# A graph layer's message stage in a written order, with its statistics taken by pairs of PSUM banks

## The chip, the cores and the metric

The kernel runs on one core of one Trainium2 chip. Everything is float32. The metric is the device time of one execution in microseconds; 4303.69 us is the median of three runs before the change (4302.92 to 4304.81). PE is the matrix engine, PEld its weight loads, DVE the vector engine, ACT the scalar engine, POOL the GpSimd engine, and SP the engine that here only issues DMAs.

## The reference

There are 12500 nodes with 96 features and 412500 edges with four attributes, sorted by target node `dst`. A small layer makes a message for each edge, the messages are added up at their targets, and each row of the result is normalized.

```python
def _mlp(h, W, b, gamma, beta):
    h = relu(h @ W + b)
    mu = mean(h, axis=0)
    var = mean(square(h - mu), axis=0)
    return gamma * (h - mu) * rsqrt(var + EPS) + beta

node_feat = _mlp(x, W_node, b_node, g_node, beta_node)
edge_feat = _mlp(edge_attr, W_edge, b_edge, g_edge, beta_edge)
message = concatenate([x[src], x[dst], edge_feat], axis=1)       # 412500 x 288
message = _mlp(message, W_msg, b_msg, g_msg, beta_msg)
agg = segment_sum(message, dst, num_segments=12500)
out = layernorm(x + agg + node_feat)
```

The two batch normalizations over all edges need their mean and variance before anything that comes after them can be scaled. The edge one must be known before the messages; the message one can be applied at the end, to the sums.

## The kernel before

**Tables.** The product with the message weights is split in three: x times the source part gives `p_tab`, x times the target part gives `q_tab`, both tables in DRAM with 12544 rows of 96 (function `table`, lines 136 to 152). Each table is made in seven chunks of 14 matmuls; a chunk's results go to four PSUM banks, `pt`, four matmuls to a bank and two in the last. DVE and ACT copy the banks in turn into `trow`, and a DMA writes the chunk. Both tables have four `pt` buffers. ACT's queue has the four `rel_d` writes of line 200 between the two tables, and DVE works on what they write.

**Gathers.** Edges are handled in tiles of 128; four tiles are a group (512 edges, 806 groups, the last with three tiles), four groups a block (202 blocks). For each tile POOL issues one indirect DMA (line 289, `gather`), which fetches 128 rows of `p_tab` by source node. Two kinds of buffers take them. The first 26 blocks are gathered early, in two staging buffers of 16 gathers each, and SP writes each to DRAM (`spill`, line 303). Later groups go to a ring of 30 group buffers (`ahead_of`); a ring buffer is free again when DVE has added it into `hs` (line 377).

**What sets the order early on.** Lines 308 to 324 write out the order of SP and POOL by hand: four chunks of `q_tab`, spill, three chunks, three spills, then the node stage (`nodes`) with two spills in it, then the edge statistics (`edge_norm`), where four of each five load steps are followed by a spill. A staging buffer can be filled again when its spill has landed. The other three engines are ordered by a scheduler.

**Edge statistics.** For each of 202 blocks three matmuls of ten rows (line 249) make the four groups' edge features packed in 128 rows, in a PSUM tile of three banks with two buffers; ACT applies relu to all three banks at once (line 252) and DVE takes mean and variance of each bank (line 254). The three matmuls use different row groups of the array.

**Message stage.** Per block, `load` fetches edge attributes and the four 30-row windows of `q_tab` that the groups' targets fall in; `prepare` makes edge features `pr` (line 362, a matmul of six rows for each group, four banks) and from them the operand `left` (ACT line 364, DVE line 365). Per group, `message` makes `z` (line 371, four matmuls), a one-hot matrix of the targets (373), the sum with the gathered rows (377) and its relu into `h` (378); `reduce`, one group later, multiplies `h` with itself and the one-hot matrix into `pa` (386) and adds the two parts into the 30 columns of `agg` (389) and into `gram` (390). DVE and SP read the window's first column into registers in `load` (349). In this stage the scheduler orders all engines. The spilled blocks are read back (404) and stand evenly among the late ones.

**End.** From `gram` come the message mean and variance; lines 598 to 631 finish the rows.

Of the kernel before, what the change touches and what calls it, by code (L numbers as in the profile page):

```python
# [14 lines left out]
OP = mybir.AluOpType  # L15
# [39 lines left out]
RING = 30  # L55
J = 8
# [14 lines left out]
def gnn(ctx, tc, t):  # L71
# [64 lines left out]
    def table(out, w, work, ps, queues):  # L136

        rows = out.rearrange("(p b) f -> p b f", b=NB)
        for c in range(0, NB, CH):
            r = work.tile([P, CH, C], F32, name="trow", bufs=3)  # L140
            for j, i in enumerate(range(0, CH, NBK)):
                n = min(NBK, CH - i)
                pt = ps.tile([P, NBK, C], F32, name="pt", bufs=4)
                for g in range(n):
                    k = COL[c + i + g]
                    nc.tensor.matmul(pt[:, g, :], xp[:, k:k + P], w, start=True, stop=True)  # L146
                if j % 2:
                    nc.scalar.activation(r[:, i:i + n, :], pt[:, :n, :], AF.Copy)  # L148
                else:
                    nc.vector.tensor_copy(r[:, i:i + n, :], pt[:, :n, :])  # L150
            queues[c // CH % len(queues)].dma_start(rows[:, c:c + CH, :], r)
            yield

    with tc.tile_pool(name="win_w", bufs=1) as work, tc.tile_pool(name="win_ps", bufs=2, space=PSUM) as ps:
        for _ in table(p_tab, w_msg[:, 0, :], work, ps, (nc.sync, nc.scalar)):
            pass
# [77 lines left out]
    def edge_norm():  # L234

        with tc.tile_pool(name="es", bufs=2) as work, tc.tile_pool(name="es1", bufs=1) as one, \
                tc.tile_pool(name="es_ps", bufs=2, space=PSUM) as ps:
            stats = one.tile([P, NS, NBL, 6], F32, name="estats")
            for b in range(NBL):
                if b % J == 0:  # L240
                    yield
                    ea = work.tile([P, J, GE], F32, name="ea")
                    n = min(J, NBL - b)
                    for i in range(NS):
                        nc.sync.dma_start(ea[Q * i:Q * i + 2 * EK, :n, :],
                                          t["ea"][EK * i:EK * (i + 2), b:b + n, :])
                pr = ps.tile([P, NS, GE], F32, name="pr")
                for i in range(NS):
                    nc.tensor.matmul(pr[:, i, :], wide[Q * i:Q * i + 2 * EK, :],  # L249
                                     ea[Q * i:Q * i + 2 * EK, b % J, :], start=True, stop=True)  # L250
                r = work.tile([P, NS, GE], F32, name="r")
                nc.scalar.activation(r, pr, AF.Relu)  # L252
                for i in range(NS):
                    nc.vector.bn_stats(stats[:, i, b, :], r[:, i, :])  # L254
# [30 lines left out]
    def fast(ring):  # L285
# [22 lines left out]
        with tc.manual_schedule(engines={ET.SP, ET.Pool}):  # L308
            with tc.tile_pool(name="tab_w", bufs=1) as work, tc.tile_pool(name="tab_ps", bufs=2, space=PSUM) as ps:
                for i, _ in enumerate(table(q_tab, w_msg[:, 1, :], work, ps, (nc.sync,))):  # L310
                    if i in (3, 6):
                        next(store)
# [12 lines left out]

        with tc.tile_pool(name="fix", bufs=1) as fix, tc.tile_pool(name="msg", bufs=2) as work, \
# [3 lines left out]
            rhs = fix.tile([P, 2, BG, C], F32, name="rhs")  # L330
            nc.vector.tensor_copy(rhs[:C], w_e[:, None, None, :].to_broadcast([C, 2, BG, C]))
            for i in range(2):
# [5 lines left out]
            hb = [fix.tile([P, GT, P], F32, name=f"h{i}") for i in range(4)]  # L338
# [3 lines left out]
            def load(s, b):  # L342

                n = min(BG, NG - b * BG)
                ea = work.tile([P, GE], F32, name="ea")
# [4 lines left out]
                    base[:, b * BG:(b + 1) * BG], engines=[ET.DVE, ET.SP], min_val=0, max_val=N - 1,  # L350
                    skip_runtime_bounds_check_because="they are nodes' numbers")
                for i in range(n):
                    nc.sync.dma_start(rhs[C:C + WN, s % 2, i, :], q_tab[bass.ds(val[i], WN), :])
                return ea, val

            def prepare(s, b, ea):

                n = min(BG, NG - b * BG)
                x = left[s % 2]
                pr = ps.tile([C + WN, BG, GE], F32, name="pr", bufs=1)  # L360
                for i in range(n):
                    nc.tensor.matmul(pr[:, i, :], we[Q * i:Q * i + EK + 1, :],  # L362
                                     ea[Q * i:Q * i + EK + 1, :], start=True, stop=True)
                nc.scalar.activation(x[:C, :n, :], pr[:C, :n, :], AF.Relu)  # L364
                nc.vector.tensor_scalar(x[C:C + WN, :n, :], pr[C:, :n, :], 0.0, None, op0=OP.is_equal)  # L365

            def message(s, g, h, pg):
                n = min(GT, NT - g * GT)
                z = ps.tile([P, GT, C], F32, name="z")
                for i in range(n):  # L370
                    nc.tensor.matmul(z[:, i, :], left[s % 2][:KR, g % BG, i * P:(i + 1) * P],  # L371
                                     rhs[:KR, s % 2, g % BG, :], start=True, stop=True)
# [7 lines left out]
            def reduce(g, h, val):  # L380

                n = min(GT, NT - g * GT)
                pa = ps.tile([C + 1, P], F32, name="pa")
# [4 lines left out]
                to = agg[:, bass.ds(val, WN)]  # L388
# [4 lines left out]
            early, late = list(range(SPILL // BG)), list(range(SPILL // BG, NBL))  # L393
            order = []
            for i, b in enumerate(late):
                order.append(b)
                while early and (SPILL // BG - len(early)) * len(late) < i * (SPILL // BG):
                    order.append(early.pop(0))
            order += early

            def fetch(b):
                if b * BG < SPILL:
                    back = work.tile([P, BG, GT, C], F32, name="pb")
                    nc.sync.dma_start(back, spill[b].rearrange("p g (a c) -> p g a c", a=GT))
                    for i in range(BG):
                        got[b * BG + i] = back[:, i, :, :]

            ea, val = load(0, order[0])
            prepare(0, order[0], ea)
            fetch(order[0])  # L410
            last, n, ahead = None, 0, SPILL + RING
            for s, b in enumerate(order):
                more = s + 1 < len(order)
                if more:
                    ea, then = load(s + 1, order[s + 1])
                    fetch(order[s + 1])
                for g in range(b * BG, min((b + 1) * BG, NG)):
                    if g % BG == 1 and more:
                        prepare(s + 1, order[s + 1], ea)
                    h = hb[n % len(hb)]  # L420
                    n += 1
                    message(s, g, h, got.pop(g))
                    if last:
                        reduce(*last)
                    last = g, h, val[g % BG]
                    if g >= SPILL and ahead < NG:
                        got[ahead] = ahead_of(ahead)
                        ahead += 1
                val = then
            reduce(*last)  # L430
# [237 lines left out]
```

## Time and profile before

| | |
|---|---|
| median of three runs | 4303.69 us |
| the profiled execution | 5713.74 us |
| its span, first to last instruction | 5712.0 us |
| mean granted PE clock in the span | 0.656 |
| busy: PE, PEld, DVE, ACT, POOL | 3507.9, 2613.4, 1830.5, 1126.2, 3070.7 us |
| message stage, from about 1230 to 5649 us: busy PE, DVE, ACT, POOL | 2898.6, 1311.6, 774.9, 2556.7 us |
| edge statistics, from about 400 to 1230 us: busy PE, DVE, ACT, POOL | 404.0, 395.1, 292.5, 397.6 us |
| granted clock in these two | 0.67 and 0.50 |
| DMA: mean rate | 55 GB/s |

In a group row the number after x is the count, then come busy time and the mean of one in nanoseconds, then the idle time of the engine just before these instructions and what ended it ("issue": nothing that the profile shows; "remote": a semaphore whose setter it cannot name). A row of waits gives the total, how often, and the longest. A row of the timeline gives start, duration, engine, line and operation, with the idle time before it in brackets. A float32 matmul leaves two records of PE. The profiled execution is a third longer than the runs without the profiler.

### The profile page before, as it was taken

Reading aid. Unit: us, or ns where it says so; the run is one execution under the profiler, and the core shown is the slowest. Engines: PE = TensorE matmul, PEld = TensorE weight load, DVE = VectorE, ACT = ScalarE, POOL = GpSimd, SP = SyncE. Lnnn points to the kernel's source line nnn. Section 1 sums busy time; section 2 is a strip of 40 time slices with the busy share of each in tenths; the row PEclk is TensorE's granted clock in tenths of the full one; section 3 lists DMA queues with packets and bytes.
Section 4 is the critical chain, followed back from the end, with each engine's and each line's share of the span. In section 5 each row is a group of like instructions: output and inputs, shape, how many; then the busy total and the mean of one; then the engine's idle time right before and its main releaser. Section 6 shows DMA issues by size and latency. Waiting matters only on the chain. (4 is left out here: it accounts for less than half of the span.)

```text
span 5712.0 us, 52958 instructions
## 1 busy us (share of the span) xinstructions
PE 3507.9 (61%) x16561; PEld 2613.4 (46%) x16561; DVE 1830.5 (32%) x4227; ACT 1126.2 (20%) x1304; POOL 3070.7 (54%) x3231
## 2 busy tenths in 40 slices
PE   3445666146666666766667566676566666665768
PEld 3331111024545455555555455455455555554547
DVE  1134555142323223232222232232322222322326
ACT  0113444021111111111111111111111111111113
POOL 2254444725555565555565555655555655556550
PEclk9955555557776666566666766666666666666667
DMA  3232323212222222222222222222222222222212
GB/s 117 73 97 56 70 63 68 47 42 51 52 52 49 46 50 52 50 52 49 52 46 51 50 51 49 47 52 49 51 50 52 46 50 52 49 52 46 50 44 82
DMA packets 190423, 315.48 MB, mean 55 GB/s; under 512 B 95817, under 2 KB 96201, under 8 KB 189128
## 3 DMA queue, kind: packets, MB, share of 16 engines
q0 software_dynamic: 103136, 158.62, 13.2%
q1 hardware_dynamic: 83502, 141.01, 8.9%
q10 hardware_dynamic: 3496, 12.36, 0.7%
q8 instruction: 137, 2.24, 0.2%
q14 instruction: 152, 1.25, 0.1%
HBM read 270.34 MB, written 41.37 MB: 55 GB/s over the span
## 5 line engine op out<-in xcount | busy, mean ns | idle before, releaser
L289 POOL DMA_INDIRECT pg<-p_tab,src x2807 | 2670.2, 951 | 1884.8 <-issue 787.5
L371 PE MATMUL z<-rhs,left 127*128 127x96 f32 x6446 | 1330.3, 350 | 706.3 <-issue 385.0
L371 PEld LDWEIGHTS z<-rhs,left 127*128 127x128 f32 x6446 | 1181.7, 261 | 1158.2 <-issue 684.0
L386 PE MATMUL pa<-h 128*97 128x127 f32 x6446 | 1236.4, 355 | 656.2 <-issue 351.7
L386 PEld LDWEIGHTS pa<-h 128*97 128x97 f32 x6446 | 1077.7, 230 | 719.8 <-issue 377.2
L378 ACT ACTIVATE h<-hs 128x384 f32<-128x384 f32 x806 | 419.5, 521 | 3094.3 <-DVE hs L377 1528.7
L389 DVE TENSOR_TENSOR agg<-pa,agg 97x30 f32 x806 | 150.4, 187 | 1978.1 <-PE z L371 752.6
L377 DVE TENSOR_TENSOR hs<-z,pg 128x384 f32<-128x384 f32 x702 | 390.2, 556 | 1054.7 <-issue 471.4
L289 POOL DMA_INDIRECT stage<-p_tab,src x416 | 399.6, 961 | 608.1 <-DMA spill<-stage 428.3
L362 PE MATMUL pr<-ea,we 6*126 6x512 f32 x1612 | 601.4, 841 | 157.4 <-issue 102.5
L249 PE MATMUL pr<-ea,wide 10*128 10x512 f32 x1212 | 406.6, 1107 | 409.2 <-ACT r L252 264.8
L254 DVE BATCH_NORM_STATS2 estats<-r 128x6 f32<-128x512 f32 x606 | 372.1, 680 | 442.6 <-ACT r L252 287.2
L364 ACT ACTIVATE left<-pr 96x2048 f32<-96x2048 f32 x202 | 376.3, 1863 | 549.9 <-remote 260.7
L365 DVE TENSOR_SCALAR left<-pr 30x2048 f32<-30x2048 f32 x202 | 462.9, 2292 | 43.8 <-ACT left L364 37.6
L249 PEld LDWEIGHTS pr<-ea,wide 10*128 10x128 f32 x1212 | 114.5, 307 | 700.0 <-ACT r L252 484.4
L252 ACT ACTIVATE r<-pr 128x1536 f32<-128x1536 f32 x202 | 292.2, 1451 | 592.9 <-remote 384.4
L362 PEld LDWEIGHTS pr<-ea,we 6*126 6x126 f32 x1612 | 150.6, 232 | 226.0 <-issue 150.3
L373 DVE TENSOR_TENSOR h<-rel,iota 128x120 f32<-128x120 f32 x806 | 204.9, 275 | 2.4 <-issue 0.4
L390 DVE TENSOR_TENSOR gram<-pa,gram 97x97 f32<-97x97 f32 x806 | 201.8, 250 | 0.3 <-DVE agg L389 0.3
L146 PE MATMUL pt<-w_msg,xp 96*128 96x96 f32 x392 | 85.6, 423 | 139.2 <-ACT trow L148 131.4
L146 PEld LDWEIGHTS pt<-w_msg,xp 96*128 96x128 f32 x392 | 84.1, 332 | 140.5 <-ACT trow L148 132.2
L223 PE MATMUL py<-center,xp 96*128 96x96 f32 x196 | 43.1, 423 | 60.5 <-DVE y0s L227 37.5
(95 smaller groups left out, 443.5 us busy)
## 6 DMA issues: line engine op xcount, KB each, us to landing
ea<-in_eaq SPq DMA_DIRECT2D x202, 256.0 KB
pg<-p_tab,src POOLq DMA_INDIRECT x2807
spill<-stage SPq DMA_DIRECT2D x26, 768.0 KB
pb<-spill SPq DMA_DIRECT2D x26, 768.0 KB
rhs<-q_tab SPq DMA_DIRECT2D x806, 11.2 KB
ea<-in_ea SPq DMA_DIRECT2D x75, 160.0 KB
stage<-p_tab,src POOLq DMA_INDIRECT x416
q_tab<-trow SPq DMA_DIRECT2D x7, 672.0 KB
```

The lines of the kernel that those rows point to most:

```text
L249: nc.tensor.matmul(pr[:, i, :], wide[Q * i:Q * i + 2 * EK, :], ea[Q * i:Q * i + 2 * EK, b % J, :], start=True, stop=True)
L252: nc.scalar.activation(r, pr, AF.Relu)
L254: nc.vector.bn_stats(stats[:, i, b, :], r[:, i, :])
L289: nc.gpsimd.indirect_dma_start(out=pg[:, i, :], out_offset=None, in_=p_tab[:, :], in_offset=bass.IndirectOffsetOnAxis(ap=src[:, k:k + 1], ...
L362: nc.tensor.matmul(pr[:, i, :], we[Q * i:Q * i + EK + 1, :], ea[Q * i:Q * i + EK + 1, :], start=True, stop=True)
L364: nc.scalar.activation(x[:C, :n, :], pr[:C, :n, :], AF.Relu)
L365: nc.vector.tensor_scalar(x[C:C + WN, :n, :], pr[C:, :n, :], 0.0, None, op0=OP.is_equal)
L371: nc.tensor.matmul(z[:, i, :], left[s % 2][:KR, g % BG, i * P:(i + 1) * P], rhs[:KR, s % 2, g % BG, :], start=True, stop=True)
L373: nc.vector.tensor_tensor(h[:, :, C + 1:C + 1 + WN], rel[:, g, :].unsqueeze(2).to_broadcast([P, GT, WN]), iota[:, None, :].to_broadcast([P ...
L377: nc.vector.tensor_add(hs[:, :n, :], z[:, :n, :], pg[:, :n, :])
L378: nc.scalar.activation(h[:, :n, :C], hs[:, :n, :], AF.Relu)
L386: nc.tensor.matmul(pa[:, :C + 1 + WN], h[:r, i, :C + 1], h[:r, i, :C + 1 + WN], start=i == 0, stop=i == n - 1)
```

## The change

The message stage is put in an order written by hand for all five engines. Edge features of a block are made during the block before it, all four matmuls in one step (`edges`), and `left` is made from them in two halves (`prepare`). `load` runs two blocks ahead, with three `ea` and three `rhs` buffers; `h` has six buffers instead of four. `linear` makes z one group ahead. `sums` puts the sums of four groups in one PSUM bank, and `add` adds a group's sums to `agg` and `gram` five groups later (`SKEW`); DVE reads its registers there. The edge statistics take consecutive matmuls by pairs, two banks to a PSUM tile with four buffers, so that ACT works on 1024 columns at a time. The second table, `q_tab`, gets eight `pt` buffers; `p_tab` keeps four.

```diff
+SKEW = 5
+HB, RB = 6, 3
...
-    def table(out, w, work, ps, queues):
+    def table(out, w, work, ps, queues, bufs):
...
-                pt = ps.tile([P, NBK, C], F32, name="pt", bufs=4)
+                pt = ps.tile([P, NBK, C], F32, name="pt", bufs=bufs)
...
-        for _ in table(p_tab, w_msg[:, 0, :], work, ps, (nc.sync, nc.scalar)):
+        for _ in table(p_tab, w_msg[:, 0, :], work, ps, (nc.sync, nc.scalar), 4):
...
-                tc.tile_pool(name="es_ps", bufs=2, space=PSUM) as ps:
+                tc.tile_pool(name="es_ps", bufs=4, space=PSUM) as ps:
...
-                pr = ps.tile([P, NS, GE], F32, name="pr")
                 for i in range(NS):
-                    nc.tensor.matmul(pr[:, i, :], wide[Q * i:Q * i + 2 * EK, :],
+                    k = NS * b + i
+                    if k % 2 == 0:
+                        pr = ps.tile([P, 2, GE], F32, name="pr")
+                    nc.tensor.matmul(pr[:, k % 2, :], wide[Q * i:Q * i + 2 * EK, :],
                                      ea[Q * i:Q * i + 2 * EK, b % J, :], start=True, stop=True)
-                r = work.tile([P, NS, GE], F32, name="r")
-                nc.scalar.activation(r, pr, AF.Relu)
-                for i in range(NS):
-                    nc.vector.bn_stats(stats[:, i, b, :], r[:, i, :])
+                    if k % 2:
+                        r = work.tile([P, 2, GE], F32, name="r", bufs=4)
+                        nc.scalar.activation(r, pr, AF.Relu)
+                        for o in (1, 0):
+                            nc.vector.bn_stats(stats[:, (k - o) % NS, (k - o) // NS, :], r[:, 1 - o, :])
...
-                for i, _ in enumerate(table(q_tab, w_msg[:, 1, :], work, ps, (nc.sync,))):
+                for i, _ in enumerate(table(q_tab, w_msg[:, 1, :], work, ps, (nc.sync,), 8)):
...
+            def edges(s):
+
+                prs[s] = ps.tile([C + WN, BG, GE], F32, name="pr", bufs=1)
+                for i in range(min(BG, NG - order[s] * BG)):
+                    nc.tensor.matmul(prs[s][:, i, :], we[Q * i:Q * i + EK + 1, :],
+                                     eas[s][Q * i:Q * i + EK + 1, :], start=True, stop=True)
+
+            def prepare(s, i):
+
+                part = slice(i, min(i + BG // 2, NG - order[s] * BG))
+                if part.start < part.stop:
+                    pr, x = prs[s], left[s % 2]
+                    nc.scalar.activation(x[:C, part, :], pr[:C, part, :], AF.Relu)
+                    nc.vector.tensor_scalar(x[C:C + WN, part, :], pr[C:, part, :], 0.0, None, op0=OP.is_equal)
...
+            def sums(k):
+
+                g = steps[k][1]
                 n = min(GT, NT - g * GT)
-                pa = ps.tile([C + 1, P], F32, name="pa")
+                h = hb[k % HB]
+                if k % 4 == 0:
+                    pas[k // 4] = ps.tile([C + 1, 4, P], F32, name="pa")
+                pa = pas[k // 4][:, k % 4, :]
...
+            def add(k):
+                s, g = steps[k]
+                if s not in vals:
+                    b = order[s]
+                    _, vals[s] = nc.values_load_multi_w_load_instructions(
+                        base[:, b * BG:(b + 1) * BG], engines=[ET.DVE], min_val=0, max_val=N - 1,
+                        skip_runtime_bounds_check_because="they are nodes' numbers")
+                pa = pas[k // 4][:, k % 4, :]
+                to = agg[:, bass.ds(vals[s][g % BG], WN)]
                 nc.vector.tensor_tensor(to, pa[:, C + 1:C + 1 + WN], to, op=OP.add)
                 nc.vector.tensor_add(gram, pa[:, :C + 1], gram)
...
+            with tc.manual_schedule(engines={ET.SP, ET.Pool, ET.PE, ET.DVE, ET.Activation}):
+                load(0)
+                fetch(0)
+                load(1)
+                edges(0)
+                prepare(0, 0)
+                prepare(0, BG // 2)
+                linear(0)
+                for k in range(n + SKEW):
+                    s, g = steps[min(k, n - 1)]
+                    if k < n and g % BG == 0:
+                        if s + 2 < len(order):
+                            load(s + 2)
+                        if s + 1 < len(order):
+                            fetch(s + 1)
+                    if k + 1 < n:
+                        linear(k + 1)
+                    if k < n:
+                        message(k)
+                    if 0 <= k - 1 < n:
+                        sums(k - 1)
+                    if k < n and s + 1 < len(order):
+                        if g % BG == 0:
+                            edges(s + 1)
+                        if g % BG >= BG // 2:
+                            prepare(s + 1, (g % BG - BG // 2) * (BG // 2))
+                    if k >= SKEW:
+                        add(k - SKEW)
+                    if k < n and g >= SPILL and ahead < NG:
                         got[ahead] = ahead_of(ahead)
                         ahead += 1
```

## The prediction

> **What bounds the kernel now.** I read the page's busy times and groups first, then the waits of POOL, then stretches of the timeline.
>
> ```profile
> PE 3507.9 (61%) x16561; PEld 2613.4 (46%) x16561; DVE 1830.5 (32%) x4227; ACT 1126.2 (20%) x1304; POOL 3070.7 (54%) x3231
> ...
> L289 POOL DMA_INDIRECT pg<-p_tab,src x2807 | 2670.2, 951 | 1884.8 <-issue 787.5
> ...
> L289 POOL DMA_INDIRECT stage<-p_tab,src x416 | 399.6, 961 | 608.1 <-DMA spill<-stage 428.3
> ```
>
> Nothing looks full: POOL is busy for 54%. But its 2807 + 416 = 3223 gathers are one serial list, and 787.5 us of their idle time ended on "issue", on nothing. The waits say how often, and what else stopped POOL:
>
> ```profile
> POOL pg L289 <- issue: 787.5, 2499, 2.7
> POOL pg L289 <- DVE h L373: 584.2, 83, 15.6
> POOL stage L289 <- DMA spill<-stage: 428.3, 13, 137.7
> ```
>
> 787.5 / 2499 = 0.32 us before nearly every gather. In the timeline:
>
> ```profile
> 3007.30 0.95 POOL L289 DMA_INDIRECT pg<-p_tab,src  x1 [0.30 <-issue]
> 3008.55 0.95 POOL L289 DMA_INDIRECT pg<-p_tab,src  x1 [0.30 <-issue]
> 3009.80 0.95 POOL L289 DMA_INDIRECT pg<-p_tab,src  x1 [0.30 <-issue]
> ```
>
> A gather costs POOL 1.25 us from start to start. **A rule against a row**: the Trainium skill (Perfetto Trace Analysis, "GPSIMD Engine Instruction") says that the span shown for a GpSimd instruction is unreliable, and to time it by start-to-start spacing. By the row's 951 ns the gathers are 3065 us, 71% of the 4303.69 us median, and POOL has slack; by the spacing they are 3223 x 1.25 = 4029 us, 94% of it, and POOL is the bound. I take the spacing.
>
> **The profiled execution against the median.** It took 5713.74 us, 1410 more than 4303.69. POOL's list explains both. Its 33rd gather starts at 236.21; 3191 more take 3191 x 1.25 = 3989; after the last the kernel needs about 5 us for the last group (eviction 0.56, relu 0.52, sums 1.0, adds 0.44, landing about 2) and 63.5 us from the last add (5648.5) to the span's end, and 1.7 us lie around the span. That is 236 + 3989 + 5 + 63.5 + 1.7 = 4295: 9 us below the median. In the profiled execution the last gather starts at 5563, so POOL also waited 5563 - 236 - 3989 = 1338 us, and its ring of 30 groups was full, so that the end took 149 us and not 69. 1338 + 80 = 1418 is the excess of 1410, but for those 9 us. The waits come from stretches like this one, in which DVE, PE and SP stand still together and POOL alone goes on until its ring is full:
>
> ```profile
> 3003.39 0.47 DVE L373 TENSOR_TENSOR h<-rel,iota 128x120 f32<-128x120 f32 x2
> 3016.31 0.19 DVE L389 TENSOR_TENSOR agg<-pa,agg 97x30 f32 x1 [12.45 <-remote]
> ```
>
> I count these stops to the profiled execution alone: with them POOL could not have finished in 4304 us. Without gathers beside it, at the end of the stage, the message work runs free:
>
> ```profile
> 5641.85 0.55 DVE L377 TENSOR_TENSOR hs<-z,pg 128x384 f32<-128x384 f32 x1
> ...
> 5643.15 0.56 DVE L377 TENSOR_TENSOR hs<-z,pg 128x384 f32<-128x384 f32 x1 [0.29 <-PE z L371]
> ...
> 5644.94 0.56 DVE L377 TENSOR_TENSOR hs<-z,pg 128x384 f32<-128x384 f32 x1 [0.34 <-PE z L371]
> ```
>
> About 1.6 us a group, where POOL needs 4 x 1.25 = 5.0. Of 806 groups, 672 are gathered in the stage (104 come from the spill, 30 from the ring), so POOL's pace is 672 x 5.0 / 806 = 4.17 us a group. So I read the measured kernel as POOL-bound from 236 us on; the message work has to stay under 4.17.
>
> **The change part by part.**
>
> *Written order of the message stage.* The same 806 groups. PE per group, by the spacing of the records' starts in the timeline: z is 8 records at 0.111 us with the full clock granted (0.213 with half), pa 8 at 0.108 (0.211). The edge features pr come as three matmuls together and one alone now, two passes over the array of 1.06 us each (2.06 at half); the change issues all four together: one. Per group before 0.89 + 0.86 + 2 x 1.06/4 = 2.3 us (half clock 4.4), after 2.0 (3.9). All of that lies beside gathers: cost of the cut 0. Without that cover it would be worth 202 x 1.06 = 214 to 202 x 2.06 = 416 us.
>
> *Halves of left.* Two ACT operations of 1.02 (the 1024-wide form, minimum of that group) for one of 1.86: +0.18 a block; DVE 2 x 1.23 for 2.29: +0.17. 202 x 0.18 = 36 us each, on engines busy for 20% and 32%: 0; at worst 36 without cover.
>
> *Adds five groups later, four sums in a bank.* Same instructions, no new DMA; a DVE register load now stands directly before its first use (0.34 us, 202 times, 69 us beside gathers: 0). With a fixed order, what waits blocks its queue: hs(k) waits on DVE for the gather, behind it stand the half of left and the add of k-5; PE's pr of the next block waits for left's last half, and behind it z(k+2). Each is needed two groups later, 10 us at POOL's pace, and the chain is 0.52 + 1.02 + 1.23 + 1.0 = 3.8. At the end four more adds follow the last one: 4 x 0.44 = 1.8, partly under the last relu and sums: 0.3 to 1.8, I take +1.
>
> *SP.* Per block the same six DMAs and one register load, a block earlier, with a third rhs and ea buffer; 12 bias rows for 8 (4 x 0.33 us, before the stage, while the ring fills: 0). POOL's list keeps its order, and each ring gather waits for the same eviction as now.
>
> *Statistics by pairs.* ACT per 1024 columns: from 1451 ns (1536) and 1863 (2048) 0.80 ns a column, so 1.04; 303 x 1.04 = 315 against 293. DVE keeps 606 operations at 0.6 us spacing, 1.8 us a block. Before, undisturbed:
>
> ```profile
> 574.56 1.45 ACT L252 ACTIVATE r<-pr 128x1536 f32<-128x1536 f32 x1 [0.20 <-PE pr L249]
> 576.60 1.45 ACT L252 ACTIVATE r<-pr 128x1536 f32<-128x1536 f32 x1 [0.59 <-PE pr L249]
> 578.30 1.45 ACT L252 ACTIVATE r<-pr 128x1536 f32<-128x1536 f32 x1 [0.26 <-PE pr L249]
> ```
>
> Two blocks in 3.7 us, 1.85 each. Four of five load steps (8 blocks) also spill 16 gathers: 40 blocks take 74 us, POOL's 64 gathers 80. POOL sets the pace, with 8% to spare: 0.
>
> *Eight banks for the target table.* This part is on POOL's path. POOL stands from 98 to 236 us for the first spill, which SP issues after four q_tab writes:
>
> ```profile
> 74.74 6.29 PE L146 MATMUL pt<-w_msg,xp 96*128 96x96 f32 x28 [0.37 <-DVE most L188]
> ...
> 211.96 24.42 PE L146 MATMUL pt<-w_msg,xp 96*128 96x96 f32 x113 [130.93 <-ACT trow L148]
> 212.38 18.54 SPq L151 DMA_DIRECT2D q_tab<-trow  x4
> ...
> 231.21 0.33 SPq L303 DMA_DIRECT2D spill<-stage  x1
> ...
> 236.21 0.95 POOL L289 DMA_INDIRECT stage<-p_tab,src  x1 [137.68 <-DMA spill<-stage]
> ```
>
> At 74.74 PE fills its four banks (28 records, 14 matmuls, one of seven chunks) and waits until 211.96 for ACT. With eight banks it fills two chunks, so 14 matmuls fewer stand between 211.96 and the fourth write: 28 records x 0.216 us = 6.0 us. Here too a **rule and a row** differ: the skill (TensorE: Matmul & The Clock Gate, "What's actually happening") has the clock go full after about 3.4 us of sustained work; then it would be nearer 28 x 0.11 = 3.1. The row shows 113 records in 24.42 us without a break, 0.216 each to the end, so 6.0. What follows (second spill, node stage, statistics) starts 6 us sooner with it.
>
> Sum: 4303.7 - 6.0 + 1 = 4298.7; 4298.
>
> **Rivals.** A, as above: 4298, own range 4293 to 4304; 0.48. A measurement of this kernel can tell about 0.2%, 8.6 us, from no change.
>
> B, the 9 us that the sum leaves, and more if a gather is a little cheaper unprofiled, are POOL waits for slow message or statistics work, and the change removes part: 4280 to 4294, say 4289. For it: POOL waits for DVE are the profile's largest; against: they belong to the stops. 0.20.
>
> C, gathers are much cheaper unprofiled (0.95: chain 236 + 3031 + 70 = 3337) and message work at half clock is the bound: 806 x 4.4 + 750 + 65 = 4361, near the median. Then pr in one pass gives 806 x 3.9 + 815 = 3958. For it: granted clock 0.67 in the stage; against: the spacing never varies, whatever else runs. 0.10.
>
> D, slower: the pairs break the three-fold overlap of the statistics matmuls on PE. Two at a time at half clock is about 1.71 us a pair, 1.5 pairs 2.56 a block; 40 blocks take 102 us against 80 of gathers, SP's spills come late, and POOL waits 22 us in each of 4.75 such rounds: +107, 4405. It decides from 80/40 = 2.0 us a block on; at 2.1 it is 4 x 4.75 = +19, 4317. Against: with four buffers PE need not stop between pairs. 0.22.
>
> **How the numbers follow.** Faster: C, nine tenths of B and a little of A (0.15): 0.10 + 0.18 + 0.07 = 0.35. Slower is D, 0.22; the rest, 0.43, is the same. The range takes in A, B, a gather cheaper by 0.01 us with its 32 us of freed waits, and the lower third of D: 4270 to 4330.
>
> **What would show it.** Gathers still 1.25 us apart; the first POOL gather after the long wait at 230 and not 236; pr as four records side by side; less PE busy time and no shorter total. It is wrong if the spacing changes, if POOL waits for spills in the statistics grow, or if the median falls below 4270, which POOL's list forbids.

## The result, and the profile after

The changed kernel takes 4322.25 us (median of 5 runs, 4319.65 to 4325.15) against 4302.92 for the kernel before (5 runs, 4300.59 to 4304.81): a ratio of 1.0048, 95% interval 1.0036 to 1.0059. It is 19 us slower. The forecast was 4298, "the same" the likeliest; the range 4270 to 4330 held the time, the direction was wrong.

Each of the five sets of experiments below ran on one chip with the kernel before beside it, whose median was 4302 and 4313 us in two sets and 5665 to 5718 us in three, with the stretches in which DVE, PE and SP stand still, so a kernel is compared only with the kernel before of its own set.

The profile of the changed kernel is free of those stretches. Its page:

```profile
span 4323.2 us, 52620 instructions
...
PE 2815.2 (65%) x16561; PEld 2342.0 (54%) x16561; DVE 1849.7 (43%) x4430; ACT 1141.2 (26%) x1606; POOL 3068.5 (71%) x3231
...
L294 POOL DMA_INDIRECT pg<-p_tab,src x2807 | 2669.4, 951 | 855.5 <-issue 661.1
...
L294 POOL DMA_INDIRECT stage<-p_tab,src x416 | 398.2, 957 | 330.3 <-DMA spill<-stage 134.7
```

POOL's waits, to be set beside those of the kernel before in the prediction (us in all, times, longest):

```profile
POOL pg L294 <- issue: 661.1, 2169, 0.3
POOL pg L294 <- DMA pg<-p_tab,src: 143.2, 470, 0.3
POOL stage L294 <- DMA spill<-stage: 134.7, 3, 132.4
```

No wait of a `pg` gather is longer than the 0.3 us that stand between any two gathers, whatever name it carries. The waits of 584, 301 and 175 us for DVE (its operations on `h`, `gram` and `hs`) are gone: in the message stage POOL waits for nobody, and it is DVE that waits for gathers. POOL is the bound, as the prediction read it. Its start, in the timeline:

```profile
73.98 12.26 PE L148 MATMUL pt<-w_msg,xp 96*128 96x96 f32 x56 [0.37 <-DVE most L190]
...
211.29 21.01 PE L148 MATMUL pt<-w_msg,xp 96*128 96x96 f32 x97 [125.05 <-ACT trow L150]
...
224.58 0.33 SPq L308 DMA_DIRECT2D spill<-stage  x1
...
230.12 0.94 POOL L294 DMA_INDIRECT stage<-p_tab,src  x1 [132.43 <-DMA spill<-stage]
```

PE fills twice 28 records into the banks from 74 us on, and the 33rd gather starts at 230.12 where it started at 236.21: 6.1 us earlier, as forecast. So the list of gathers must have lost some 25 us after that. From the starts of the gathers in the trace: the 33rd at 230.1; 3190 spacings of 1.25 are 3987.5; gathers 34 to 416 (spill, beside the statistics) took 20.3 in all beyond 1.25 each, the ring's and the message stage's 16.1; the last gather starts at 4254.0 and the span ends 69.2 later. 230.1 + 3987.5 + 20.3 + 16.1 + 69.2 = 4323.2, the span. For the kernel before, taken at its median (a span of 4301.2) and with the same end, the sum leaves 4301.2 - 236.2 - 3987.5 - 69.2 = 8.3 us for both excesses together. About 28 us more than before went into gathers and gaps that the prediction had at exactly 1.25. Less the 6.1 of the start that is 22 us; the profiled execution is 2.6 us over its median, so 19 of them are the difference of the medians.

In the message stage the edge features do go in one pass, as the timeline shows (8 records, four matmuls, 1.14 us; before, two passes):

```profile
2002.21 1.14 PE L386 MATMUL pr<-ea,we 6*126 6x512 f32 x8 [0.79 <-DVE left L395]
```

### The profile page after: what moved, and what is told of

It reads as the page before. It is cut to its first block, busy times and chain, and to the rows that moved or that the text cites. A ratio compares the mean times of both kernels' runs of the same rounds, so it can differ in the third digit from the quotient of the medians.

```text
span 4323.2 us, 52620 instructions
## 1 busy us (share of the span) xinstructions
PE 2815.2 (65%) x16561; PEld 2342.0 (54%) x16561; DVE 1849.7 (43%) x4430; ACT 1141.2 (26%) x1606; POOL 3068.5 (71%) x3231
## 5 line engine op out<-in xcount | busy, mean ns | idle before, releaser
L294 POOL DMA_INDIRECT pg<-p_tab,src x2807 | 2669.4, 951 | 855.5 <-issue 661.1
L402 PE MATMUL z<-rhs,left 127*128 127x96 f32 x6446 | 1139.7, 334 | 1237.7 <-issue 844.4
L402 PEld LDWEIGHTS z<-rhs,left 127*128 127x128 f32 x6446 | 1032.0, 243 | 1480.5 <-issue 905.2
L426 PE MATMUL pa<-h 128*97 128x127 f32 x6446 | 1066.8, 321 | 4.7 <-ACT h L414 4.7
L426 PEld LDWEIGHTS pa<-h 128*97 128x97 f32 x6446 | 950.1, 206 | 5.2 <-ACT h L414 5.2
L395 DVE TENSOR_SCALAR left<-pr 30x1024 f32<-30x1024 f32 x403 | 495.7, 1230 | 638.9 <-ACT left L394 638.9
L394 ACT ACTIVATE left<-pr 96x1024 f32<-96x1024 f32 x403 | 403.5, 1001 | 15.5 <-DMA rhs<-q_tab 14.2
L257 ACT ACTIVATE r<-pr 128x1024 f32<-128x1024 f32 x303 | 294.9, 1024 | 163.2 <-PE pr L253 133.2
L253 PEld LDWEIGHTS pr<-ea,wide 10*128 10x128 f32 x1212 | 205.0, 317 | 207.9 <-issue 92.7
L386 PE MATMUL pr<-ea,we 6*126 6x512 f32 x1612 | 232.0, 644 | 20.3 <-DMA ea<-rel_d 10.5
L438 DVE TENSOR_TENSOR agg<-pa,agg 97x30 f32 x806 | 149.7, 186 | 26.7 <-PE pa L426 2.2
L386 PEld LDWEIGHTS pr<-ea,we 6*126 6x126 f32 x1612 | 62.9, 182 | 53.3 <-DVE left L395 21.7
```

The source lines that it names most:

```text
L253: nc.tensor.matmul(pr[:, k % 2, :], wide[Q * i:Q * i + 2 * EK, :], ea[Q * i:Q * i + 2 * EK, b % J, :], start=True, stop=True)
L294: nc.gpsimd.indirect_dma_start(out=pg[:, i, :], out_offset=None, in_=p_tab[:, :], in_offset=bass.IndirectOffsetOnAxis(ap=src[:, k:k + 1], ...
L386: nc.tensor.matmul(prs[s][:, i, :], we[Q * i:Q * i + EK + 1, :], eas[s][Q * i:Q * i + EK + 1, :], start=True, stop=True)
L394: nc.scalar.activation(x[:C, part, :], pr[:C, part, :], AF.Relu)
L395: nc.vector.tensor_scalar(x[C:C + WN, part, :], pr[C:, part, :], 0.0, None, op0=OP.is_equal)
L402: nc.tensor.matmul(zs[k][:, i, :], left[s % 2][:KR, g % BG, i * P:(i + 1) * P], rhs[:KR, s % RB, g % BG, :], start=True, stop=True)
```

## The experiments

### One part at a time, and more gathers

Four kernels made from the kernel before. Eight banks alone:

```diff
-                pt = ps.tile([P, NBK, C], F32, name="pt", bufs=4)
+                pt = ps.tile([P, NBK, C], F32, name="pt", bufs=bufs)
...
-                for i, _ in enumerate(table(q_tab, w_msg[:, 1, :], work, ps, (nc.sync,))):
+                for i, _ in enumerate(table(q_tab, w_msg[:, 1, :], work, ps, (nc.sync,), 8)):
```

> The kernel before with one part of the change: eight banks for pt while the target table is made. Theory (POOL's list of gathers sets the time): the first POOL gather after the long wait comes 6 us earlier (230.1 in the profile of the changed kernel, 236.2 before), all that follows moves with it, -6 us. If the start was no gain for the end: 0. Its profile also shows the old message stage and old statistics once more: if the 1410 us by which the profiled execution before exceeded the median belong to that one execution, they are not there this time (span about 4297); if the old message stage draws them in every profiled execution, they are.

The pairs of banks alone (`edge_norm` of the changed kernel), and the message stage alone (the rest of the diff):

> The kernel before with one part of the change: edge statistics by pairs of banks. The changed kernel is 19 us slower although its start gained 6, so 25 us have to be found. Theory P: they are in the statistics, where the profile of the changed kernel has 18 us of gaps in POOL's list (gathers 97 to 416): +18 to +25. Theory M: they are in the message stage: 0 here. Rival D of the prediction, rounds that wait for spills: +19 or more.

> The kernel before with the message stage of the changed kernel alone (written order, edge features a block ahead, four sums in a bank, adds five groups later; old statistics, four banks). Theory M: +25 us, from gathers that take longer on POOL: the changed kernel's profile has some 160 gathers of 1.04 to 1.13 us for 0.94, 14 to 17 us in all, beside the adds on DVE. Theory P: 0 to +7. By the prediction's own step: +1.

And 88 gathers more:

```diff
         def ahead_of(g):
+            if g % 8 == 0:
+                again = ring.tile([P, C], F32, name="again", bufs=4)
+                nc.gpsimd.indirect_dma_start(
+                    out=again, out_offset=None, in_=p_tab[:, :],
+                    in_offset=bass.IndirectOffsetOnAxis(ap=src[:, g * GT:g * GT + 1], axis=0))
             return gather(g, ring.tile([P, GT, C], F32, name="pg"))
```

> The kernel before with 88 more gathers, one before every eighth group from group 104 on, into a tile of their own that nothing reads. If POOL's list sets the time and a gather costs 1.25 us: +110 us. If a gather costs its span of 0.95: +84. If the message work on PE and DVE sets it (rival C): 0 to +20.

In this set the kernel before took 5703.27 us (27 runs). Eight banks: 5695.75, ratio 0.9989 (0.9981 to 0.9997), 7.5 us less. Pairs: 5667.94, 0.9937 (0.9918 to 0.9955), 35 less. Message stage: 5650.76, 0.991 (0.9889 to 0.9931), 52 less. More gathers: 5818.02, 1.0202 (1.0182 to 1.0221), 115 more, or 1.30 a gather. With eight banks alone POOL waits for DVE as in the profiled execution before, 604 us for `h` and 278 us for `gram`.

So the stretches are no matter of that one profiled execution: all 27 timed runs have the longer time too. And since POOL waits for DVE in them, these four runs tell nothing of the 19 us. Only the earlier start could be read: the 33rd gather at 230.7 with eight banks, at 236.0 (pairs) and 235.4 (message stage) without them.

### Each part taken out of the changed kernel, and an earlier first spill

The changed kernel with the old statistics; with the old message stage; and itself once more:

> The changed kernel with the old edge statistics (three banks at a time, two buffers). In the first four runs the kernel before itself took 5703 us and its profile had the stretches in which DVE, PE and SP stand still together; there the pairs alone were worth -35 us and the message stage alone -52. If the stretches are absent (the kernel before near 4303), theory P expects this kernel at about the kernel before less 6, and theory M expects it near the changed kernel, +19. If they are present, parts that add up give -6 - 52 = -58.

> The changed kernel with the old message stage. Without the stretches: theory M expects -6 (only the earlier start is left), theory P expects +19. With them: -6 - 35 = -41 if the parts add up.

> The changed kernel again, beside the three others and the kernel before of this call. Without the stretches +19 us, as measured; with them -6 - 35 - 52 = -93 if the three parts add up.

In this set the kernel before took 4312.5 us (17 runs). The changed kernel took 4338.09, ratio 1.0059 (1.0045 to 1.0072): +25.6. With the old statistics 4331.25, 1.0044 (1.003 to 1.0057): +18.8. With the old message stage 4316.3, 1.0009 (1.0 to 1.0017): +3.8. By difference the pairs cost 25.6 - 18.8 = 6.8 us, the message stage 25.6 - 3.8 = 21.8, and what is left for the banks is 25.6 - 6.8 - 21.8 = -3 (the trace has the start 5 to 6 earlier). The 6.8 are no larger than the intervals, but no run of the changed kernel (4335.29 to 4341.39) lies as low as one with the old statistics (4323.7 to 4333.51). So theory M (message stage) has most of it, theory P (pairs) a part.

The traces say where. The gathers' group, of the changed kernel again and then with the old message stage:

```profile
L294 POOL DMA_INDIRECT pg<-p_tab,src x2807 | 2680.2, 955 | 855.9 <-issue 755.3
```

```profile
L292 POOL DMA_INDIRECT pg<-p_tab,src x2807 | 2653.5, 945 | 855.5 <-issue 778.4
```

The same 2807 gathers are busy for 26.7 us more; the idle time between them is equal (855.9 and 855.5). With the old message stage PE is busy for 3351.0 us, in the changed kernel for 2835.5: the cut of 515 us is real, and bought nothing. Of the 2807 gathers 170 last longer than 1.0 us, 34 with the old stage. What the lengthened gathers take beyond the median gather is 25.0 us with the change and 5.0 with the old stage: 20.0 of the 26.7. The other 6.7 are 2 to 3 ns on every gather (median 0.947 for 0.944 us) and no work of the written order, for the first trace of the changed kernel has 0.944 too (there the lengthened ones are 20.7 us). In the timeline, POOL and DVE of the changed kernel:

```profile
2066.93 0.19 DVE L438 TENSOR_TENSOR agg<-pa,agg 97x30 f32 x1
2067.04 0.25 DVE L439 TENSOR_TENSOR gram<-pa,gram 97x97 f32<-97x97 f32 x1
2067.16 1.13 POOL L294 DMA_INDIRECT pg<-p_tab,src  x1 [0.30 <-DVE agg L438]
2067.20 0.27 DVE L409 TENSOR_TENSOR h<-rel,iota 128x120 f32<-128x120 f32 x1
...
2068.60 0.95 POOL L294 DMA_INDIRECT pg<-p_tab,src  x1 [0.30 <-issue]
```

The gather at 2067.16 has the comparison of `rel` with `iota`, which makes the one-hot matrix, running from 2067.20 to 2067.47, and takes 1.13; the next one takes 0.95. Counted over all 2807 gathers of this trace, by what DVE does 0.15 us after the gather's start (two operations can overlap in the records; with the comparison there, the gather stands in the first row):

| DVE at that moment | gathers | longer than 1.0 us |
|---|---|---|
| the comparison (`rel`, `iota`) | 201 | 170 |
| nothing | 1647 | 0 |
| `hs` | 437 | 0 |
| half of `left` | 393 | 0 |
| `agg` or gram add | 98 | 0 |
| others | 31 | 0 |

So it is not the adds, as theory M had it. In every one of the 170 the gather's end comes 0.812 to 0.822 us after the comparison's end, wherever in the gather the comparison began; the later it starts, the longer the gather, from 1.02 us where it starts 0.05 to 0.10 before the gather to 1.16 where it starts 0.05 to 0.10 after. Fifteen more in the first row are lengthened to less than 1.0 us, with the same distance. The 16 that are not lengthened have the comparison starting 0.11 us or more after them. So the gather seems to have a step some 0.13 us after its start (0.944 - 0.817) that waits for the comparison's end, if the comparison is there first.

Other operations of DVE run beside the early gathers, far from any comparison. In the first trace of the changed kernel:

```profile
62.14 3.53 DVE L178 TENSOR_TENSOR rel<-dsti,basei 128x3232 f32<-128x3232 int32 x1 [11.85 <-DMA basei<-in_base]
62.43 4.05 POOL L294 DMA_INDIRECT stage<-p_tab,src  x1 [0.30 <-issue]
65.70 3.52 DVE L181 TENSOR_REDUCE worst<-rel 128x1 f32<-128x3232 f32 x1
66.79 0.94 POOL L294 DMA_INDIRECT stage<-p_tab,src  x1 [0.31 <-issue]
68.04 0.95 POOL L294 DMA_INDIRECT stage<-p_tab,src  x1 [0.30 <-issue]
```

The subtraction that makes `rel` has both inputs in SBUF; the gather beside it takes 4.05 us and ends 0.81 us after it. The reduction, as long, has one input in SBUF, and the gathers beside it take 0.94 and 0.95. So do the 281 gathers that meet a `bn_stats` of the edge statistics, again with one input in SBUF, while all ten that meet the node stage's operation on `xp` (line 219, 1.51 us, `agg` and `xp` both in SBUF) take 1.12 to 1.74 us and end 0.82 us after it. The trace with the old message stage has three comparisons in a row up to 766.83 us and beside them a gather of 1.68 us, which ends 0.82 us after the third. What the lengthening operations share is two inputs in SBUF. One case has a single input: the copy of `w_e` into `rhs` (768 columns in 0.56 us, with the old message stage) made one gather 1.14 us long, again to 0.82 us after its end; the changed kernel's copy (1152 columns in 1.35 us) lengthened none.

The statistics' share is in POOL's waits between 260 us and the first ring gather, first with the old statistics, then of the changed kernel:

```profile
POOL stage L291 <- DMA stage<-p_tab,src: 10.9, 10, 1.7
POOL stage L291 <- DMA spill<-stage: 2.1, 1, 2.1
```

```profile
POOL stage L294 <- DMA stage<-p_tab,src: 20.4, 21, 2.3
POOL stage L294 <- DMA spill<-stage: 2.1, 1, 2.1
```

POOL does not wait longer for spills (rival D's place); it waits 9.5 us more for what the profile names as earlier gathers that have yet to land. Gathers 34 to 416 exceed 1.25 each by 14.1 us in all with the old statistics; with the pairs by 21.4 here, and by 20.3, 19.8 and 17.6 in the traces of the first run of the change, of the old message stage and of the comparison moved (below). So the pairs cost 3.5 to 7 us there. Why the gathers land later with them was not tried.

The fourth kernel starts the list earlier, by the order on SP alone:

```diff
-SPILL = 26 * BG
+SPILL = 30 * BG
...
+            for _ in range(7):
+                next(store)
```

> The kernel before with seven spills put ahead of the target table's writes in SP's list, and 30 blocks spilled for 26: POOL no longer stands from 98 to 236 us for the first spill. If POOL's list sets the end: about -125 to -133 us (the wait of 137.7, less a few us). If it is something in the message stage (PE, DVE, or the stretches in which they stand still), whose start does not move: 0 to -30, the latter for four more blocks that the stage finds gathered.

4253.92 us, ratio 0.9867 (0.9852 to 0.9882): 59 us less, half of what was expected. The 33rd gather starts at 97.4, but SP's row of the third spill, between the loads of the relative targets, lasts from 121.3 to 152.1, and POOL stands 21 us from 137 and 48 us from 178 for spills. A wait taken from one place on POOL came back from SP's list.

### The comparison moved

If a gather's length hangs on when the comparison runs, moving this one operation must bring back the time, with everything else of the change in place. It now stands behind `hs` of the group before, ahead of the half of `left` and the adds:

```diff
             def message(k):
...
-                nc.vector.tensor_tensor(
-                    h[:, :, C + 1:C + 1 + WN], rel[:, g, :].unsqueeze(2).to_broadcast([P, GT, WN]),
-                    iota[:, None, :].to_broadcast([P, GT, WN]), op=OP.is_equal)
                 hs = work.tile([P, GT, C], F32, name="hs", bufs=3)
                 nc.vector.tensor_add(hs[:, :n, :], z[:, :n, :], pg[:, :n, :])
+                onehot(k + 1)
                 nc.scalar.activation(h[:, :n, :C], hs[:, :n, :], AF.Relu)
```

> The changed kernel with one operation of DVE's list moved: the comparison that makes the one-hot columns of group k+1 (rel against iota, both in SBUF) is issued directly behind hs of group k, ahead of the half of left and the two adds, and no longer behind the gram add. Theory W: a gather is lengthened (0.94 to some 1.08 us) when this comparison runs 0.15 to 0.20 us after the gather's start, as it did in all 165 long gathers of the last trace of the changed kernel; the move takes it away from there by 0.4 to 1.7 us. Expected: under 60 long gathers, 12 to 22 us less than the changed kernel, 3 to 13 over the kernel before. Rival: DVE's adds do it, or any operation of DVE at that moment; then the adds now stand 0.27 us later, in the gather's first 0.2 us, and the number of long gathers stays at 160 or rises; time no better than the changed kernel's +22 to +25.

A second kernel makes it twice:

> The changed kernel with the same comparison made twice in a row for each group, 806 operations of 0.27 us more on DVE, which is idle for half of the stage. Theory W: the second one reaches 0.25 us further into the next gather, the number of long gathers rises from 165 to 250 or more and the time to +30 or more over the kernel before. Rival (the comparison is not the cause): DVE has room, the time stays at +22 to +25.

Two more put the first seven spills into POOL's own list, again with 30 blocks spilled, from the kernel before (with eight banks) and from the changed kernel with the comparison moved:

```diff
-SPILL = 26 * BG
+SPILL = 30 * BG
+EARLY = 7
...
+            held = None
             for b in range(SPILL // BG):
                 pg = ring.tile([P, BG, GT, C], F32, name="stage", bufs=2)
                 for i in range(BG):
                     gather(b * BG + i, pg[:, i, :, :])
+                    if i == 0 and held is not None:
+                        nc.gpsimd.dma_start(spill[b - 1], held)
+                        held = None
+                if b < EARLY:
+                    held = pg.rearrange("p g a c -> p g (a c)")
+                else:
+                    nc.sync.dma_start(spill[b], pg.rearrange("p g a c -> p g (a c)"))
+                    yield
```

> The kernel before with the eight banks, 30 blocks spilled for 26, and the first seven spills issued from POOL's own list, each four gathers into the next block, so that no spill stands in SP's list behind the relative targets. With the seven spills in SP's list the gain was 59 us and POOL still stood 22 and 49 us; here POOL should not stand from 98 to 236 us at all: -137 us, plus some 7 x 1.2 us for issuing seven spills: about -125. If the message stage starts later or waits for work because of it, less.

> The changed kernel with both: the comparison moved behind hs, and the early spills from POOL's list with 30 blocks. Theory W and POOL's list: within 15 us of the kernel before with the early spills (that is, -110 to -130 against the kernel before).

The kernel before took 5717.63 us here (9 runs), so the times answer nothing on the 22 us: moved 5614.27, ratio 0.9821 (0.9808 to 0.9834); twice 5613.5, 0.9825 (0.9812 to 0.9838); spills on POOL 5641.79, 0.9867 (0.9852 to 0.9883); both 5559.6, 0.9728 (0.9714 to 0.9741). The traces still say something. Moved: 63 long gathers, all 63 with the comparison at 0.15 us; of 215 with the gram add there and 311 with `hs`, none. That speaks against the rival that any operation of DVE at that moment lengthens a gather. Made twice: 199 long ones, fewer than the 250 expected.

Two of them once more:

> The changed kernel with the comparison moved behind hs once more. In the last four runs the kernel before took 5718 us, with stretches in which PE issues one matmul in 0.7 us and POOL waits for DVE, so that the end did not hang on single gathers; what could be seen there is that 63 gathers were long, all 63 with the comparison 0 to 0.2 us after their start, and none with the adds there. If the kernel before is near 4303 here: theory W expects the changed kernel's +22 to +25 to fall to +3 to +13; the rival (written order as such, whatever stands next to a gather) expects +19 or more. If it is near 5700: -100 again, and nothing is told apart.

> The changed kernel with the comparison moved and the first seven spills in POOL's own list (30 blocks spilled). If the kernel before is near 4303: -110 to -130, since POOL no longer stands from 98 to 236 us. If it is near 5700: -158 again.

The kernel before took 4301.52 us here (17 runs). With the comparison moved 4303.62, ratio 1.0005 (0.9997 to 1.0014): +2.1 where the changed kernel had +19 and +26. The gathers' group and a piece of the timeline of it:

```profile
L294 POOL DMA_INDIRECT pg<-p_tab,src x2807 | 2651.8, 945 | 855.5 <-issue 658.0
```

```profile
2037.56 0.95 POOL L294 DMA_INDIRECT pg<-p_tab,src  x1 [0.30 <-issue]
2037.62 0.56 DVE L417 TENSOR_TENSOR hs<-z,pg 128x384 f32<-128x384 f32 x1 [3.92 <-DMA pg<-p_tab,src]
2038.09 0.27 DVE L407 TENSOR_TENSOR h<-rel,iota 128x120 f32<-128x120 f32 x1
```

945 ns a gather again, 2651.8 us in all. `hs`, which reads `z` in PSUM and one operand in SBUF, starts 0.06 us after the gather and the gather takes 0.95; the comparison follows 0.53 us after its start and harms nothing. 25 gathers are long, and the lengthened ones take 3.0 us in all beyond the median. Of the message stage's 22 us nothing measurable is left, so by difference its written order, the sums of four groups in a bank and the late adds cost nothing by themselves; the place of one comparison did.

With the early spills as well 4192.66, ratio 0.9749 (0.9735 to 0.9762), 109 us less than the kernel before:

```profile
102.74 0.94 POOL L295 DMA_INDIRECT stage<-p_tab,src  x1 [0.30 <-issue]
103.69 0.58 POOL L311 DMA_DIRECT2D spill<-stage  x1
104.57 0.97 POOL L295 DMA_INDIRECT stage<-p_tab,src  x1 [0.30 <-issue]
...
256.81 0.94 POOL L295 DMA_INDIRECT stage<-p_tab,src  x1 [12.34 <-DMA spill<-stage]
```

A spill issued by POOL costs its list 1.83 - 1.25 = 0.58 us, and POOL goes on; it stands once more, 12.3 us, for the first spill that SP issues. The 33rd gather starts 130.2 us earlier than with the comparison moved alone (99.0 for 229.2), the last 110.2 earlier (4122.7 for 4232.9), and the time is 111 lower. This shows that the list of gathers sets the end.

### The last four

> The changed kernel with the comparison moved, the old statistics, and the first eight spills (not seven) in POOL's own list, 30 blocks spilled. The run before it of this kind was -109; there POOL still stood 12.3 us for the spill of the eighth block, and the pairs of banks cost some 6 us: -122 to -130, if the kernel before is near 4303.

> The changed kernel with the comparison moved and the old statistics: the message stage in its written order and the eight banks alone. Theory W and the 6 us of the statistics: -4 to -6 against the kernel before. If the pairs cost nothing: +2, as with the comparison moved alone.

> The changed kernel with the comparison made twice in a row, once more, for a kernel before near 4303. On the chip with the stretches it had 198 long gathers (63 with the comparison moved), 22.6 us of lengthening: theory W +25 to +35 over the kernel before, no less than the changed kernel's +19 to +25. Rival: as the changed kernel, +19 to +25, with no more than 165 long gathers.

> The kernel before with 88 more gathers, once more, for a kernel before near 4303: POOL's list expects +110 (88 x 1.25), a gather of 0.95 expects +84. Near 5700 it was +115, where POOL also waited for DVE.

The kernel before took 5665.05 us here (9 runs). All joined: 5521.9, ratio 0.9744 (0.9726 to 0.9763). Comparison moved, old statistics: 5561.89, 0.9822 (0.9805 to 0.984). Comparison twice: 5567.78, 0.983 (0.9814 to 0.9845), with 150 long gathers, again not more than in the changed kernel. The expected growth of the count with a second comparison did not come; perhaps because it also shifts when everything behind it runs, which was not tried. More gathers: 5786.94, 1.022 (1.0203 to 1.0236), 122 us or 1.39 a gather, more than its 1.25. So it stays open whether the changed kernel with the comparison moved and the old statistics ends below the kernel before where that takes 4302 us (by difference -5), and what one more gather costs the total there was not measured by itself.

## Why the prediction was wrong, step by step

**What bounds the kernel: right.** POOL's list of 1.25 us gathers; the changed kernel's trace has no wait of POOL for DVE in the message stage, and starting the list 130 us earlier took 111 us off.

**The stops belong to the profiled execution alone: wrong.** The 27 timed runs of the kernel before in one set took 5703 us. The sum came out all the same because the median to be forecast was taken where the stops are absent. Their cause is open, and nothing tried here removes them. In those sets the message stage alone took 52 us off and the pairs 35, and the kernels nearest to the changed one, with the comparison moved or doubled, are 97 to 104 us faster than the kernel before; the changed kernel itself was not run there.

**Eight banks, -6.0: right.** The 33rd gather starts 6.1 us earlier; in time -7.5 in one set and -3 by difference in another. The 6.0 rest on the row's 0.216 us a record. Whether that is the clock is not on record: the trace of before has its first clock entry at 264 us, behind these matmuls (its rows read 1.00 until then). The spacing fits half the clock, since the `py` matmuls of the same shape run at 0.21 us a record with 0.50 granted (271 to 283 us in the changed kernel's trace).

**Statistics by pairs, 0: undersized.** The pace of the blocks did hold: three pairs are two blocks, 3 x 1.185 = 3.56 us between their starts, 1.78 a block (1.71 with the old statistics, the prediction's view had 1.85), below the 2.0 from which rival D decides, and POOL's waits for spills did not grow. Rival D's 1.71 us a pair was too high. But POOL waited 9.5 us more for its own gathers to land, and the time rose by 6.8.

**The written message stage, +1: the step that failed.** The prediction put DVE's work beside the gathers at 0, because every gather was to cost POOL 1.25 us: "the spacing never varies, whatever else runs", and "POOL's list keeps its order". The order was kept, but DVE can lengthen a gather without any wait in the program: the part measured +21.8 us, and 16 to 20 of them are lengthened gathers in the two traces. The Trainium skill has the rule (SBUF — State Buffer, "Who interferes with whom"): a DVE instruction with two inputs in SBUF contends with a GpSimd instruction that reads SBUF, since its second input comes by the interface that the two share. A gather reads its row numbers (`src`) from SBUF, and of DVE's operations on a group the comparison of `rel` with `iota` alone has both inputs there; the others read PSUM. This case agrees: 170 of the 201 gathers with the comparison at 0.15 us are longer than 1.0 us and none of the others, and the subtraction and the operation on `xp`, with two inputs in SBUF too, did the same. The inputs' places were not varied by themselves in one operation.

The comparison is not new; only its place is. In the order that the scheduler chose, it stood at 0.15 us of a gather 57 times (trace with the old message stage), 33 of these gathers long; more than half of the 806 comparisons started 0.4 to 0.9 us after a gather's start, where they harm nothing. The written order put it behind the gram add, where it starts at nearly every point of POOL's 1.25 us and met a gather's start 201 times. With the comparison moved by one place, the whole change measured +2.1 instead of +19 and +26, each against the kernel before beside it.

**The 9 us that the sum left.** Rival B took them for POOL's waits that the change would partly remove. Waits beyond 1.25 exist in the statistics (14.1 us in gathers 34 to 416 with the old statistics), and the change added to them.

**The signs and the shares.** The signs that the prediction named came true (the spacing's median, the earlier 33rd gather, four records side by side, less PE time and no shorter total) while the time rose: a median of 1.25 does not show that one gather in fourteen is longer. "Slower" had 0.22, all of it rival D. That D's lower end, 4317, is near the 4322 measured, and that the range held the time, is luck: the mechanism is another, and no case for the message stage ended on that side. The trace before had the evidence, unread: 68 gathers over 1.0 us in the message stage, all with the comparison at 0.15 us.

## What to carry to other kernels

Where one engine's serial list is the bound, ask not only who makes it wait but who makes its single operations longer: compare the group's mean with its minimum (955 ns for 941 in the changed kernel run again), and look at what runs beside the long ones. When an order is written out, an operation that shares something with the bounding engine has to be placed against that engine's rhythm; here one comparison behind `hs` and not behind the adds was worth some 20 us. And a long wait of the bounding engine at the start can be worth more than cuts on the other engines: of 132 us of waiting for one spill, 111 came off with seven spills in POOL's own list, where a cut of 515 us on PE bought nothing.

## What the runs showed of the hardware

- A gather of 128 rows takes POOL 1.25 us from start to start (median 1.249 to 1.252 in every trace), 0.94 of it shown as busy.
- A gather that meets a DVE operation with two inputs in SBUF about 0.13 us after its start ends 0.82 us after that operation's end: 1.2 us at most with one comparison of 0.27 us, 4.05 us with a subtraction of 3.53 us. Operations with an input in PSUM (`hs`, half of `left`, the adds) and `bn_stats` and the reduction, with one input in SBUF, lengthened none.
- Where the comparison stands directly behind `hs`, 92 gathers had it at 0.15 us, 35 were lengthened and 25 of them long. In the other 57 the record of `hs` runs to 0.05 us or more past the gather's start, so the comparison may have begun to read later than its record shows; that was not tried.
- A spill of 768 KB issued by POOL took 0.58 us of its list.
